# Four selective-scan layers on one core: the side steps of layer 0 in other groups, and one weight set loaded during the first step

## The chip, the core and the metric

The kernel runs on one core of a Trainium2 chip. A core has a matrix engine (PE, with its weight loads shown as PEld), a vector engine (DVE), a scalar engine (ACT), a general engine (POOL) and a queue that issues transfers (SP); each works through its own list of instructions in the order of the program, and they wait for one another through semaphores. The metric is the device time of one execution in microseconds (us), the median of several runs.

## The reference, cut to what matters

Four layers follow one another on images of 192 channels and 48 by 48 pixels, four images, all in 32-bit floats. The change is in layer 0. For each image it runs two pairs of Mamba passes; in a pair one pass reads the 2304 pixels forward, the other backward, and their results are added:

```
xz = u @ inW.T;  xh, z = split(xz);  xc = silu(causal_conv(xh, 3 taps))
xdbl = xc @ xpW.T          # dt (12), B (16), C (16)
delta = softplus(dt @ dtW.T + dtB);  A = -exp(A_log)
h_t = exp(delta_t*A) * h_(t-1) + (delta_t*u_t) * B_t      # 16 states x 384 channels
y_t = sum_n h_t*C_t + xc*D;  out = (y * silu(z)) @ outW.T
layer 0:  m = pair_0(x with rows and columns swapped)
          out = pair_2(layernorm(m swapped back)*w + b + x)
```

Between the two pairs each pixel is normalised over its 192 channels and the input is added. This "mixing" is what the text calls the side steps. Layers 1 to 3 (a convolution block with a four-direction scan, another four-direction scan, a row-wise and column-wise Mamba with an MLP) are not touched by the change.

## The kernel before, in words

**Jobs, steps and groups.** A pass of layer 0 over one image is cut into 6 jobs of 384 pixels (`MambaJob`, `mamba_pass`). Layer 0 has 2 pairs x 4 images x 2 directions x 6 = 96 jobs, and `run_jobs` takes them one after another in one long pipeline. The 384 channels are 3 blocks of 128, the 16 states are 4 groups of 4, so a job has 12 groups; "step n" is the stretch in which the groups of job n are scanned, and "group 0" to "group 11" is the place in it (the variable `at`). One group on DVE is a multiplication `inputs<-du,bcb` and the scan `h<-a,inputs`.

**Who feeds the scan.** ACT makes the decays `a` two groups ahead, into three buffers that rotate, so its four exponentials of group t start when the scan of group t-1 has ended. In groups 3, 7 and 11 it also copies the next channel block's `du` into PSUM, after three of the four exponentials; the next `inputs` on DVE reads that copy. POOL multiplies the scanned `h` by C (`h<-h,bcb`). PE then adds it up in PSUM (`y<-h,ident`, `reduce`), one group later. `h` has three buffers: the scan of group t+3 writes over that of group t.

**Work for the neighbours.** Beside these, a step projects the next job (`units` of `MambaJob`: `inner` and `conv` in groups 0 to 3, B and C in group 5, `delta` in group 7, `z` in groups 9 and 10), and closes the previous one: its output projection in groups 4 and 6, and for a backward job the sum with the forward pass's result (`o<-o,prior`, on POOL, group 8). Each such unit is a PE part and an ACT part with a PSUM buffer of two (`ps`) between them. The functions silu and softplus are in other ACT tables than exp, so these units are framed by table loads.

**Side steps.** `mix` makes, for each backward job of the first pair, a list of steps from `Normed.norm`: two centerings (`ps<-o,center` on PE, then on ACT a copy `nx<-ps` and a square `nsq<-ps`), the variance (`ps<-nsq,mean` on PE, then Ln and Exp on ACT), a scaling on POOL, a load of the input, an affine pair on ACT, and an addition into the turned image on POOL. `Side.slot` starts at most one of them per group, when the group is in the list for its kind; `run_jobs` offers a job's list in group `offered` of the step after the next job's start, and calls `Side.slot` after the units and ahead of `reduce`. So the places of the side steps in each engine's list follow from `offered` and `slots`. There are 24 such jobs, one per backward chunk and image, and their side steps lie in the first half of layer 0.

**Weights.** `PairWeights` holds one direction's weights. `load` issues 7 transfers on SP; `derive` makes `A` and 12 diagonal matrices of 128x128. With `late` false these are DVE instructions; with `late` true they are ACT instructions, handed to a job as `extras` (`load` in group 0, `A` and four matrices in group 8, four in group 9, four in group 11). Before the change both sets of the first pair are loaded and derived ahead of everything, and the second pair's two sets are extras of later jobs.

Of the kernel before, what the change touches and what calls it, by code (L numbers as in the profile page):

```python
# [33 lines left out]
def halves(d):  # L34

    return d.rearrange("(k p) l -> p k l", p=Q)
# [251 lines left out]
class ScanJob:  # L288
# [8 lines left out]
    steps, offered = None, 3  # L297
# [200 lines left out]
class MambaJob(ScanJob):  # L498
# [2 lines left out]

    skips, offered = True, 9

    def __init__(
        self, k, pools, w, c0, rev, prev, src, dst, mirror=False, twin=None, prior=None
# [404 lines left out]
def mamba_pass(k, pools, w, rev, src, dst, mirror=False, prior=None):  # L912
    jobs = []
    for n in range(NCH):
        c0 = (NCH - 1 - n if rev else n) * CH
        prev = jobs[-1] if jobs else None
        jobs.append(MambaJob(k, pools, w, c0, rev, prev, src, dst, mirror, prior=prior))
    return jobs
# [12 lines left out]
def layer0(k, pairs, wh, norm, outs):  # L931

    with ExitStack() as ctx:
        nc = k.nc
        pool = ctx.enter_context(k.tc.tile_pool(name="w", bufs=1))
        one = ctx.enter_context(k.tc.tile_pool(name="s1", bufs=1))
        ws = [[PairWeights(k, pool, p, n, m == 1) for n, p in enumerate(pair)] for m, pair in
              enumerate(pairs)]  # L940
        for w in ws[0]:
            w.load()
            w.derive()
        nw = k.tile(one, [Q, 2, 2], "nw")
        nc.sync.dma_start(nw, norm.rearrange("(k p) v -> p k v", p=Q))
        normed = Normed(k, one, one)
        pools = ScanPools(k, ctx, 1, False)
        slots = {"pe": (1, 9, 11), "pool": (3, 7), "act": (5,), "dma": (0, 4, 8)}
        side = Side(k, pools.ps, slots)
        mixed = [k.dram([C, L], "mixed") for _ in range(B)]  # L950

        def mix(b, job):

            at = L - CH - job.c0
            c = at // CH
            st = {}

            def affine(x, of):
                st["x"] = x
                for m in range(2):  # L960
                    of(x[:, m, :], m)

            def load(sq):
                st["res"] = sq
                nc.sync.dma_start(sq, halves(wh[b])[:, :, at : at + CH])

            def add():
                for m in range(2):
                    k.g.tensor_tensor(
                        rows_of(normed.turned[:, m, :], c),  # L970
                        *(square_rows(st[v][:, m, :]) for v in ("x", "res")),
                        ALU.add,
                    )

            steps = normed.norm(
                lambda: [job.o], 0, nw[:, :, 0], nw[:, :, 1], affine, spare=load
            )
            steps.append(("pool", add))
            return [steps, *(normed.parts(halves(mixed[b]), normed.turned) if c == NCH - 1 else [])]

        jobs = []
        for m, (there, back) in enumerate(ws):
            for b in range(B):
                src = (wh, mixed)[m][b]
                first, out = k.dram([C, L], "first"), outs[b] if m else k.dram([C, L], "sum")
                some = mamba_pass(k, pools, there, False, src, first)
                some += mamba_pass(k, pools, back, True, src, out, True, first)
                if m == 0:
                    for job in some[NCH:]:
                        job.steps = lambda b=b, job=job: mix(b, job)  # L990
                jobs += some

        n = len(jobs) // 2
        for i in range(2):
            jobs[n + i * NCH - NCH + 1].extras = ws[1][i].extras()
        run_jobs(jobs, side)
# [297 lines left out]
def square_rows(ap):  # L1294

    return ap.rearrange("p (r l) -> p r l", l=S)


def rows_of(img, c):

    return img.rearrange("p (w h) -> p h w", h=S)[:, c * RC : (c + 1) * RC, :]
# [338 lines left out]
def network(tc, d, out):  # L1640
    with ExitStack() as ctx:
# [13 lines left out]

        x1 = images("x1")
        layer0(k, [pair(0), pair(2)], [d["x_wh"][b] for b in range(B)], d["L0_norm"], x1)


# [173 lines left out]
```

## Time and profile before

| what | us |
|---|---|
| median of 3 runs (19716.89 to 19721.89) | 19721.09 |
| the profiled execution's own time | 19716.54 |
| its span, from the first instruction to the last | 19714.8 |
| DVE busy | 18084.7 |
| PE busy | 17500.7 |
| POOL busy | 14746.4 |
| ACT busy | 12837.2 |
| first scan of layer 0 starts at | 42.72 |

The profile is of one execution. A busy share is an average over stages with different limits, so the text goes by single groups: the trace's answers give for an instruction its start, its length and, in brackets, the idle time of its engine just before it and what ended that idle time. "DVE inputs <- ACT du" means that `inputs` on DVE waited for the copy of `du` on ACT. Several instructions that follow one another on an engine are shown as one line with a count.

### The profile page before, as it was taken

How to read it: one execution, taken by the hardware profiler on the slowest of the kernel's cores; microseconds unless marked ns; L12 is line 12 of the kernel's file. 1: busy time of each engine (PE TensorE's matmuls, PEld its weight loads, DVE VectorE, ACT ScalarE, POOL GpSimd, SP SyncE). 2: the span in 40 equal slices, each digit the busy share in tenths (PEclk: the TensorE clock that was granted, in tenths of full speed). 3: DMA queues.
4: the chain of work that ended last, by engine and by line, in shares of the span. 5: the costliest groups of instructions: out<-in, count | busy, mean ns of one | idle time of the engine just before them, and what ended most of it. 6: DMA issues, size and time to landing. Idle time of an engine off the chain costs nothing.

```text
span 19714.8 us, 159611 instructions
## 1 busy us (share of the span) xinstructions
PE 17500.7 (89%) x48240; PEld 8295.6 (42%) x48240; DVE 18084.7 (92%) x7310; ACT 12837.2 (65%) x22569; POOL 14746.4 (75%) x10860
## 2 busy tenths in 40 slices
PE   8999999999998878888888888889999999999989
PEld 4444444444444322232233333334444444444444
DVE  8999999999998699999999999969999999999993
ACT  6666667666665466666666766766666666666663
POOL 7888878878776278888888888857777777777770
PEclk9999999999999989999999999999999999999999
DMA  3333333333332366666666666642222322333221
GB/s 113 115 108 116 110 117 117 110 114 106 112 115 88 97 134 138 149 144 148 146 143 145 140 144 144 139 115 105 105 102 105 108 105 104 111 107 106 105 106 46
DMA packets 500475, 2306.35 MB, mean 117 GB/s; under 512 B 76664, under 2 KB 334304, under 8 KB 347168
## 3 DMA queue, kind: packets, MB, share of 16 engines
q1 hardware_dynamic: 499616, 2296.14, 41.2%
q8 instruction: 387, 6.34, 0.1%
q14 instruction: 472, 3.87, 0.1%
HBM read 2103.60 MB, written 192.32 MB: 116 GB/s over the span
## 4 chain that ended last, share of the span: by engine, by line
DVE 39%; POOL 33%; PE 13%; issue 10%; ACT 3%; DMA 2%; DVEq 0%; SPq 0%; POOLq 0%; ACTq 0%
POOL h L56 25%; DVE h L56 25%; DVE inputs L56 13%; PE y L56 5%; PE ps L56 4%; POOL dus L56 3%; PE vps L114 2%; POOL state L56 1%; ACT a L93 1%; DMA bcb<-bc 1%; POOL yt L56 1%; POOL bcb L56 1%; PE mop L114 1%; PE mps L114 1%; ACT L93 1%
## 5 line engine op out<-in xcount | busy, mean ns | idle before, releaser
L56 POOL TENSOR_TENSOR h<-h,bcb 128x1536 f32<-128x1536 f32 x3456 | 11907.7, 3446 | 1704.9 <-DVE h L56 1429.9
L56 DVE TENSOR_TENSOR_SCAN h<-a,inputs 128x1540 f32<-128x1540 f32 (+1 forms) x3456 | 11606.6, 3358 | 440.6 <-ACT a L93 4.1
L93 ACT ACTIVATE a<-delta,A 128x384 f32<-128x384 f32 (+1 forms) x13824 | 7432.2, 602 | 3160.3 <-DVE h L56 3148.7
L56 PE MATMUL y<-h,ident 128*128 128x384 f32 x18432 | 6789.3, 516 | 513.5 <-POOL h L56 510.5
L56 DVE TENSOR_TENSOR inputs<-du,bcb 128x1540 f32<-128x1540 f32 (+1 forms) x3456 | 6114.4, 1769 | 503.7 <-ACT du L93 96.4
L56 PEld LDWEIGHTS y<-h,ident 128*128 128x128 f32 x18432 | 3633.6, 201 | 3517.3 <-POOL h L56 951.9
L56 PE MATMUL y<-h,sum 128*64 128x384 f32 x9216 | 3667.1, 547 | 581.4 <-POOL h L56 461.3
L56 PEld LDWEIGHTS y<-h,sum 128*64 128x64 f32 x9216 | 1292.4, 150 | 2909.0 <-issue 1738.0
L56 POOL COPY state<-h 128x4 f32<-128x4 f32 x2304 | 431.4, 187 | 2228.2 <-DVE h L56 2199.7
L56 PE MATMUL ps<-xh,diag 128*128 128x384 f32 x4032 | 1418.7, 491 | 177.9 <-ACT xc L93 177.9
L56 PE MATMUL ps<-u,inT 96*128 96x384 f32 x3456 | 1249.1, 492 | 155.1 <-ACT z L93 105.9
L56 PE MATMUL ps<-bcd,dtT 12*128 12x384 f32 (+1 forms) x2304 | 1023.8, 552 | 397.4 <-ACT delta L93 394.8
L56 PEld LDWEIGHTS ps<-xh,diag 128*128 128x128 f32 x4032 | 750.4, 189 | 772.7 <-ACT xc L93 266.0
L93 ACT ACT_TABLE_LOAD x794 | 1018.7, 1283 | 14.0
L90 ACT ACT_TABLE_LOAD x789 | 1012.3, 1283 | 14.3 <-PEq L1823 0.7
L56 PEld LDWEIGHTS ps<-u,inT 96*128 96x128 f32 x3456 | 649.4, 191 | 661.6 <-ACT z L93 177.6
L93 ACT ACTIVATE delta<-ps,vec 128x384 f32<-128x384 f32 x1152 | 630.3, 578 | 303.4 <-PE ps L56 296.9
L56 PEld LDWEIGHTS ps<-bcd,dtT 12*128 12x128 f32 (+1 forms) x2304 | 383.7, 192 | 965.8 <-ACT delta L93 631.8
L56 PE MATMUL ps<-yt,outT 128*96 128x384 f32 x2304 | 789.7, 486 | 0.4 <-POOL yt L56 0.4
L93 ACT ACTIVATE du<-dus 128x384 f32<-128x384 f32 x1152 | 558.8, 485 | 164.2 <-DVE inputs L56 158.8
L56 POOL TENSOR_TENSOR dus<-delta,xc 128x384 f32<-128x384 f32 x576 | 574.7, 998 | 51.8 <-ACT delta L93 51.8
L93 ACT ACTIVATE o<-ps 96x384 f32<-96x384 f32 x288 | 140.0, 486 | 684.4 <-PE ps L56 684.4
(131 smaller groups left out, 9702.8 us busy)
## 6 DMA issues: line engine op xcount, KB each, us to landing
bcb<-bc SPq DMA_DIRECT2D x384, 1540.0 KB
bcb<-bc SPq DMA_DIRECT2D x768, 770.0 KB
bcb<-bc SPq DMA_DIRECT2D x384, 1536.0 KB
y<-o SPq DMA_DIRECT2D x192, 288.0 KB
xs<-xi_wh SPq DMA_DIRECT2D x96, 288.0 KB
xs<-xi_hw SPq DMA_DIRECT2D x96, 288.0 KB
added<-y SPq DMA_DIRECT2D x96, 288.0 KB
xs<-x_wh SPq DMA_DIRECT2D x96, 288.0 KB
```

The lines of the kernel that those rows point to most:

```text
L56: return lambda *a, **kw: self.tc.keep_in_program_order(op(*a, **kw))
L90: self.in_order(self.nc.scalar.preload_act_table_set(LOG_EXP))
L93: return self.in_order(self.nc.scalar.activation(out, in_, func, **kw))
L114: (engine or self.nc.tensor).matmul(out, lhsT, rhs, start=start and i == 0, stop=stop and i == n - 1)
```

## The change

Two edits, both in layer 0.

The side steps move: a job's list is offered in group 11 of the step and not in group 9, and steps that begin on PE may start in groups 1, 2 and 11 and not in 1, 9 and 11. The first centering goes from group 9 to group 11, the second from group 11 to group 1 of the next step, the variance from group 1 to group 2. The scaling (group 3), the load (4), the affine pair (5) and the addition (7) stay.

The weights move: of the first pair, only the forward direction's set is loaded and derived ahead of the first job. The backward direction's set becomes `late`, and its `load` and `derive` are extras of the very first job.

```diff
-    skips, offered = True, 9
+    skips, offered = True, 11
...
-        ws = [[PairWeights(k, pool, p, n, m == 1) for n, p in enumerate(pair)] for m, pair in
-              enumerate(pairs)]
-        for w in ws[0]:
-            w.load()
-            w.derive()
+        ws = [
+            [PairWeights(k, pool, p, n, m + n > 0) for n, p in enumerate(pair)]
+            for m, pair in enumerate(pairs)
+        ]
+        ws[0][0].load()
+        ws[0][0].derive()
...
-        slots = {"pe": (1, 9, 11), "pool": (3, 7), "act": (5,), "dma": (0, 4, 8)}
+        slots = {"pe": (1, 2, 11), "pool": (3, 7), "act": (5,), "dma": (0, 4, 8)}
...
         n = len(jobs) // 2
+        jobs[0].extras = ws[0][1].extras()
         for i in range(2):
             jobs[n + i * NCH - NCH + 1].extras = ws[1][i].extras()
```

In the built program the 7 transfers of the second set stand on SP behind the first two loads of `u` and ahead of `bc<-bcd`; DVE has 13 instructions fewer at the start; on ACT the one Exp of the start goes to the first step, and 13 come to it there.

## The prediction

> **What bounds the kernel.** I read the page first: DVE is busy 92% of the span and carries most of the chain that ended last, through `h` and `inputs`.
>
> ```profile
> span 19714.8 us, 159611 instructions
> DVE 39%; POOL 33%; PE 13%; issue 10%; ACT 3%; DMA 2%; DVEq 0%; SPq 0%; POOLq 0%; ACTq 0%
> ```
>
> In layer 0 DVE sets the pace: a group takes 5.35 us, 1.77 of `inputs` and 3.36 of scan. A gain can only come from DVE's idle time, so next I asked for the waits of DVE in the first half of layer 0, 38 to 3263 us, where the side steps lie.
>
> ```profile
> DVE inputs L56 <- ACT du L93: 78.3, 25, 26.0
> DVE inputs L56 <- POOL bcb L56: 21.8, 58, 0.5
> DVE h L56 <- PE y L56: 1.8, 4, 0.5
> ```
>
> One of the 25 waits for `du` is the kernel's start (25.95 us); the other 24 hold 52.3 us, and there are 24 jobs with side steps. In the second half of layer 0, without side steps, the same view lists no wait for `du`. What makes `du` late is in the timeline of one such step (POOL, PE, ACT, DVE, by start):
>
> ```profile
> 677.52 1.80 POOL L56 TENSOR_TENSOR o<-o,prior 96x768 f32<-96x768 f32 x1
> 679.37 1.53 PE L56 MATMUL ps<-o,center 96*96 96x384 f32 x4 [3.30 <-POOL o L56]
> 681.78 4.05 PE L56 MATMUL y<-h,ident 128*128 128x384 f32 x8
> 681.00 0.49 ACT L93 ACTIVATE nx<-ps 96x384 f32<-96x384 f32 x1 [4.96 <-PE ps L56]
> 691.78 0.47 ACT L93 ACTIVATE du<-dus 128x384 f32<-128x384 f32 x1
> 692.34 1.77 DVE L56 TENSOR_TENSOR inputs<-du,bcb 128x1540 f32<-128x1540 f32 x1 [2.23 <-ACT du L93]
> ```
>
> The first centering stands in group 9, but POOL adds up the `o` that it reads behind the `h` of group 8, until 679.32. PE waits 3.30 us, ACT behind it 4.96 us, with the decays and the `z` of group 10 queued behind `nx`. ACT never recovers by group 11, and `du` is 2.23 us late for DVE.
>
> The measure of a step without side steps is one of the second half, around its groups 11 to 3:
>
> ```profile
> 6031.48 2.85 PE L56 MATMUL y<-h,ident 128*128 128x384 f32 x8 [1.21 <-POOL h L56]
> 6047.64 2.85 PE L56 MATMUL y<-h,ident 128*128 128x384 f32 x8 [0.56 <-POOL h L56]
> 6031.06 0.47 ACT L93 ACTIVATE du<-dus 128x384 f32<-128x384 f32 x1
> 6033.06 2.14 ACT L93 ACTIVATE a<-delta,A 128x384 f32<-128x384 f32 x4 [0.99 <-DVE h L56]
> 6043.85 2.13 ACT L93 ACTIVATE a<-delta,A 128x384 f32<-128x384 f32 x4 [2.32 <-DVE h L56]
> 6049.20 1.63 ACT L93 ACTIVATE a<-delta,A 128x384 f32<-128x384 f32 x3 [3.22 <-DVE h L56]
> 6033.23 1.77 DVE L56 TENSOR_TENSOR inputs<-du,bcb 128x1540 f32<-128x1540 f32 x1 [0.20 <-DVE h L56]
> ```
>
> Here `du` ends 1.5 us before the previous scan does, and both PE and ACT have idle time in front of groups 0 to 3. Last, the start: two weight sets on SP ahead of `u`, and PE's first matmul waiting for `u`.
>
> ```profile
> 4.31 0.49 SPq L824 DMA_DIRECT2D xpT<-in_L_xpT  x1
> 9.48 0.82 SPq L523 DMA_DIRECT2D u<-in_x_wh  x2
> 15.02 1.62 PE L56 MATMUL ps<-u,inT 96*128 96x384 f32 x2 [15.02 <-DMA u<-in_x_wh]
> ```
>
> **What the Trainium skill says.** "PSUM — Partial Sum Buffer", section "Engine vs sequencer instructions": the queues of ScalarE, VectorE and GpSimdE are strict FIFO and matmuls start in program order. The trace agrees: decays whose buffer was free at 679.2 start at 681.76, behind `nx`. "TensorE: Matmul & The Clock Gate", section "What's actually happening": an idle window of about 3.4 us halves the array's clock. After the 3.30 us of idle the same eight matmuls took 4.05 us, against 2.75 elsewhere, so the wait costs PE more than itself. "ScalarE: Activation LUTs", section "Table sets": one set holds both ln and exp. In this trace the Ln and Exp of the variance have no table load around them, so moving them adds none.
>
> **The change part by part.**
>
> *The centering leaves group 9.* PE's wait (3.30) and ACT's (4.96) go. ACT then starts group 10's decays at 679.25 and not at 681.76, a gain of 2.5 us; `nx` and `nsq` leave group 9 as well (0.9), and `z` finds its two PSUM buffers unshared. In the measure step `du` is in time with 1.5 us to spare. DVE's next release is then the end of its own scan, with the 0.20 us gap of that step: each of the 24 waits of 52.3/24 = 2.18 shrinks to 0.20, 24 x 1.98 = 47.5 us. In four of these steps the scan of group 10 is also held, by POOL's `state` and PE's late `y` (5.80, 5.78, 5.78 and 5.65 us for the group, not 5.37): 1.5 us more. Sum 49.
>
> *Centering in group 11.* PE: 1.45 us, in the measure step's 1.21 us of idle ahead of `reduce`. ACT: `nx` 0.48 and `nsq` 0.48, in the 0.99 us of idle. The second centering stood there before with the same size. Cost nothing; without the cover, 0.3 us on PE, which has a slack of some 3 us before an `h` buffer is needed.
>
> *Second centering in group 1, variance in group 2.* Group 1 exchanges four matmuls for four (1.45 each) and Ln/Exp (0.58+0.52) for `nx`/`nsq` (0.96). New is group 2: PE 1.45, ACT 1.10. By the measure step: the centering pushes group 1's `reduce` by about 0.5 us (0.37 of idle absorbs the rest), the variance ends near 6048.8, group 2's `reduce` is 1.0 late after its 0.56 of idle, Ln and Exp run 6048.9 to 6050.0. The queue behind them on ACT is group 3's decays, due at 6049.20: 0.8 late. `du` of group 3 then ends near 6052.0, and the scan that it must beat ends at 6054.52: 2.5 us to spare. After the table load the first `xc` is 0.5 late, and PE's third conv with it; `reduce` of group 2 then ends near 6059.3, and the scan that needs its `h` buffer starts at 6061.90. In the built program the second conv waits for the Ln that empties its PSUM buffer, which is already done, so it doesn't queue behind `xc`. Cost nothing; if that cover is used up, each us beyond 2.5 costs 24.
>
> *Queues passed.* POOL's scaling in group 3 now has one group, not two, after Exp; it stands behind the `h` of group 3, which ends near 6058.3, 8 us after Exp. On SP no transfer moves. POOL's own overload in groups 3 and 7 (the 21.8 us) stays.
>
> *The start.* SP drops seven issues ahead of `u`: 4.57 us (from 4.31 to the next transfer at 8.88). What must land ahead of `u` falls by one set, 981 KB or 1.0 MB; from 5 to 15 us the DMA moved some 240 GB/s, so 4.2 us. Bounds: 3.4 us at the 297 GB/s of its best slice, 4.6 by the issues; I take 4.2, as all of the chain to the first scan at 42.72 hangs on the first matmul. The set's transfers then run beside the first projections; SP has nothing to issue from 10.3 to 29.47.
>
> *The late set.* ACT gets 0.23+0.24+12 matrices, 4.6 us, in groups 8, 9 and 11 of the first step. The second pair's set does the same at 3307.58 to 3324.92 in the trace: `du` ended at 3323.21, `inputs` came at 3324.72 with a 0.20 gap. Cost 0. DVE's 13 instructions were off the path: 0.
>
> **Sum.** 47.5 + 1.5 + 4.2 = 53 us. The span goes from 19714.8 to 19661.6, the profiled execution from 19716.54 to 19663. That execution is 4.6 below the median of the runs; 19721 - 53 = **19668**. Of the kernel, 0.27%. About 0.2%, 39 us, is what a measurement of this kernel can tell from no change.
>
> **Rivals.**
>
> *The wait moves to group 3.* In a step with side steps PE is nearly gapless (65.6 of 71.3 us), fuller than the measure step. If PE stays as far behind as before, the variance ends 16.9 us after group 0's `inputs` began, Exp at 18.1, `du` at 20.4, against a scan end at 21.4. One us of slack then; two us more of lag would cost 24 and give 19692. For it: the full PE. Against: the lag came from the idle and the slow clock that go.
>
> *The late `du` is the table loads' doing.* Group 10's `z` with two loads of 1.28 us stands before `du` in every step; then only the start counts: 19717. Against: the measure step has the same loads and is in time.
>
> *Slower.* Ln and Exp hold group 3's decays so long that `du` stalls DVE by more than the change saves: from 53/24 = 2.2 us per step it is no gain, and from 3.8 us it is slower by 39 us, 19760. Exp would have to end 3.8+1.0 to 3.8+2.5 us later than worked. Nothing in the trace is that late there.
>
> **Chances.** The forecast 0.76 (its own range 19656 to 19679), the wait that moves 0.14 (19680 to 19712), table loads 0.06, slower 0.04. Faster by over 0.2% takes the forecast and a little of the second: 0.79; within 0.2%: 0.17; slower 0.04. The range reaches into the second case, to 19692; below, to the start's and the noise's end, 19655.
>
> **What would show it.** In the changed profile: no `nx` wait of 5 us on ACT, no PE wait for POOL `o`, DVE's waits for `du` down to the start's one of about 21.7 us, group 11 at 5.44 us, first scan near 38.5. Waits of DVE for `du` at group 3 or for PE `y` at group 5 would prove me wrong.

## The result

The changed kernel takes **19681.04 us** (median of 17 runs, 19673.69 to 19687.33) against 19720.92 for the kernel before beside it (17 runs, 19714.20 to 19727.93). The ratio is 0.998, 95% interval 0.9973 to 0.9986: 39.9 us faster, with an interval of some 28 to 53 us. The forecast was 53 us faster.

The page of the changed kernel, its span and the chain that ended last by engine:

```profile
span 19683.5 us, 159587 instructions
DVE 43%; POOL 26%; PE 15%; issue 8%; ACT 5%; DMA 1%; DVEq 1%; POOLq 0%; SPq 0%; ACTq 0%
```

The chain still runs through DVE, with a larger share than the 39% of before. Next the same view as in the prediction, the waits of DVE from 38 to 3263 us (total, times, longest, in us):

```profile
DVE inputs L56 <- POOL bcb L56: 22.5, 59, 0.5
DVE inputs L56 <- DVE h L56: 7.7, 37, 0.4
DVE inputs L56 <- POOL state L56: 2.6, 6, 0.5
DVE h L56 <- ACT a L93: 2.4, 3, 1.7
...
DVE h L56 <- PE y L56: 0.4, 1, 0.4
```

No wait for `du` is left in this window, where there were 24 with 52.3 us; POOL's `bcb` is as before (21.8 us, 58 times). The waits of `inputs` for DVE's own scan, most of them the 0.20 us gap that the prediction named, are 37 and not 21 (4.2 us before). The timeline of the same step, groups 9 to 11, shows why:

```profile
670.79 1.83 POOL L56 TENSOR_TENSOR o<-o,prior 96x768 f32<-96x768 f32 x1
672.58 2.13 ACT L93 ACTIVATE a<-delta,A 128x384 f32<-128x384 f32 x4 [1.30 <-DVE h L56]
676.03 1.06 ACT L93 ACTIVATE z<-ps 128x384 f32<-128x384 f32 x2
677.96 2.75 PE L56 MATMUL y<-h,ident 128*128 128x384 f32 x8
678.15 1.77 DVE L56 TENSOR_TENSOR inputs<-du,bcb 128x1540 f32<-128x1540 f32 x1
678.67 1.28 ACT L90 ACT_TABLE_LOAD   x1
680.55 1.45 PE L56 MATMUL ps<-o,center 96*96 96x384 f32 x4
681.50 0.47 ACT L93 ACTIVATE du<-dus 128x384 f32<-128x384 f32 x1
682.42 0.47 ACT L93 ACTIVATE nx<-ps 96x384 f32<-96x384 f32 x1
683.45 2.13 ACT L93 ACTIVATE a<-delta,A 128x384 f32<-128x384 f32 x4 [0.19 <-DVE h L56]
683.62 1.77 DVE L56 TENSOR_TENSOR inputs<-du,bcb 128x1540 f32<-128x1540 f32 x1 [0.20 <-DVE h L56]
```

POOL's `o` is complete at 672.62; the centering that reads it now starts at 680.55, without a wait. ACT's decays of group 10 begin as soon as DVE has released their buffer. `du` ends at 681.97, and DVE's `inputs` follows its own scan with a gap of 0.20 us, where it had waited 2.23.

Then the groups that took in the moved work, 1 to 3 of the following step:

```profile
693.12 0.48 ACT L93 ACTIVATE nsq<-ps 96x384 f32<-96x384 f32 x1
697.69 1.46 PE L56 MATMUL ps<-nsq,mean 96*96 96x384 f32 x4
699.25 0.58 ACT L93 ACTIVATE nsq<-ps,eps 96x384 f32<-96x384 f32 x1 [2.86 <-PE ps L56]
699.86 0.53 ACT L93 ACTIVATE nsq<-nsq 96x384 f32<-96x384 f32 x1
700.28 1.61 ACT L93 ACTIVATE a<-delta,A 128x384 f32<-128x384 f32 x3
701.56 3.36 DVE L56 TENSOR_TENSOR_SCAN h<-a,inputs 128x1540 f32<-128x1540 f32 x1
701.80 0.47 ACT L93 ACTIVATE du<-dus 128x384 f32<-128x384 f32 x1
705.06 1.77 DVE L56 TENSOR_TENSOR inputs<-du,bcb 128x1540 f32<-128x1540 f32 x1
```

Exp (the second `nsq` on ACT after 699) ends at 700.39, and `du` at 702.27, 2.65 us ahead of the end of the scan at 704.92. `inputs` at 705.06 waits for nothing.

Last the start:

```profile
4.83 0.94 SPq L523 DMA_DIRECT2D u<-in_x_wh  x2
5.82 0.45 SPq L824 DMA_DIRECT2D xpT<-in_L_xpT  x1
11.08 6.67 PE L56 MATMUL ps<-u,inT 96*128 96x384 f32 x12 [11.08 <-DMA u<-in_x_wh]
39.47 3.36 DVE L56 TENSOR_TENSOR_SCAN h<-a,inputs 128x1540 f32<-128x1540 f32 x1 [1.73 <-ACT a L93]
```

`u` is issued at 4.83 and not at 9.48, ahead of the second set (`xpT` at 5.82), and the first matmul comes 3.94 us earlier.

That is what was meant, and yet the whole is 13 us short of the forecast. To find where, I cut each span at the first and last scan of layer 0, of layers 1 and 2, and of layer 3. The cuts are the starts of these scans. There are two traces of each kernel; the second is among the experiments below:

| part, us | before | after | mean difference |
|---|---|---|---|
| to the first scan | 42.7, 43.1 | 39.5, 38.8 | -3.8 |
| layer 0, first to last scan | 6247.7, 6243.0 | 6201.6, 6201.0 | -44.1 |
| to the first scan of layer 1 | 476.8, 478.4 | 476.7, 477.3 | -0.6 |
| layers 1 and 2 | 6219.3, 6215.7 | 6225.7, 6227.6 | +9.2 |
| to the first scan of layer 3 | 164.3, 168.2 | 168.6, 167.1 | +1.6 |
| layer 3 | 6102.4, 6103.6 | 6111.6, 6111.0 | +8.3 |
| after the last scan | 461.6, 460.9 | 459.9, 460.7 | -1.0 |

Layer 0 and the start give nearly what was worked out. Some 17 us are lost in layers 1 to 3, whose code is the same in both kernels. In layer 3 the waits of DVE say where. This view of the kernel before, from just after layer 3's first scan to its last:

```profile
DVE h L56 <- ACT a L93: 0.5, 1, 0.5
```

and of the changed kernel, in the same stretch:

```profile
DVE h L56 <- ACT a L93: 3.9, 8, 0.5
DVE h L56 <- DVE inputs L56: 2.9, 6, 0.5
DVE inputs L56 <- DVE h L56: 2.3, 5, 0.5
DVE h L56 <- PE ps L56: 1.0, 2, 0.5
DVE h L56 <- PE y L56: 0.5, 1, 0.5
```

One stop became 22, each of 0.44 to 0.50 us. They are put down to ACT, to PE and to DVE itself, so no single one of these can be behind them; the releaser named is whatever ended last before. One of them in the timeline of DVE in the changed kernel:

```profile
13205.50 1.77 DVE L56 TENSOR_TENSOR inputs<-du,bcb 128x1536 f32<-128x1536 f32 x1
13207.40 3.35 DVE L56 TENSOR_TENSOR_SCAN h<-a,inputs 128x1536 f32<-128x1536 f32 x1
13210.79 1.77 DVE L56 TENSOR_TENSOR inputs<-du,bcb 128x1536 f32<-128x1536 f32 x1
13213.04 3.35 DVE L56 TENSOR_TENSOR_SCAN h<-a,inputs 128x1536 f32<-128x1536 f32 x1 [0.48 <-PE ps L56]
```

From the end of the second `inputs` to its scan are 0.48 us, where the first pair has 0.13; the stop costs the difference, 0.35. I compared these places with DVE's list of instructions in the built program, semaphore instructions included. All 22 stand at an index that leaves 64 when divided by 128, and so does the single stop of before. Both kernels pass such an index every 128 instructions, 37 times in layer 3; what differs is what stands there:

| layer 3, at such an index | before | after |
|---|---|---|
| scans, with a stop | 1 of 1 | 17 of 17 |
| multiplications, with a stop | 0 of 11 | 5 of 7 |
| semaphore instructions | 25 | 13 |

At a semaphore instruction no idle time of DVE shows, and at a multiplication it may or may not; a scan always shows it, in layers 0 to 2 too. The change takes 13 instructions from DVE's start (14988 become 14975), so every later instruction has another index.

### The profile page after: what moved, and what is told of

It reads as the page before. It is cut to its first block, busy times and chain, and to the rows that moved or that the text cites. A ratio compares the mean times of both kernels' runs of the same rounds, so it can differ in the third digit from the quotient of the medians.

```text
span 19683.5 us, 159587 instructions
## 1 busy us (share of the span) xinstructions
PE 17478.0 (89%) x48240; PEld 8281.7 (42%) x48240; DVE 18085.6 (92%) x7297; ACT 12836.3 (65%) x22582; POOL 14746.8 (75%) x10860
## 4 chain that ended last, share of the span: by engine, by line
DVE 43%; POOL 26%; PE 15%; issue 8%; ACT 5%; DMA 1%; DVEq 1%; POOLq 0%; SPq 0%; ACTq 0%
DVE h L56 28%; POOL h L56 20%; DVE inputs L56 15%; PE y L56 7%; PE ps L56 5%; POOL dus L56 2%; ACT a L93 2%; PE vps L114 2%; POOL state L56 1%; ACT L93 1%; PE mop L114 1%; DMA bcb<-bc 1%; POOL yt L56 1%; PE mps L114 1%; POOL bcb L56 1%
## 5 line engine op out<-in xcount | busy, mean ns | idle before, releaser
L90 ACT ACT_TABLE_LOAD x789 | 1012.3, 1283 | 14.7 <-PEq L1825 0.7
```

The source lines that it names most:

```text
L90: self.in_order(self.nc.scalar.preload_act_table_set(LOG_EXP))
```

## The experiments

**Theory A**: layer 0 and the start gain what was worked out, and the loss in layer 3 goes by the index of DVE's instructions. **Theory B**: the loss comes from elsewhere, such as the changed start or the changed timing of layer 0. Beside the first four runs the kernel before took 19720.59 us (38 runs); beside the next four 19718.13 (44 runs).

### The side steps alone

```diff
-    skips, offered = True, 9
+    skips, offered = True, 11
-        slots = {"pe": (1, 9, 11), "pool": (3, 7), "act": (5,), "dma": (0, 4, 8)}
+        slots = {"pe": (1, 2, 11), "pool": (3, 7), "act": (5,), "dma": (0, 4, 8)}
```

> The kernel before with the side steps moved alone (offered in group 11, PE groups 1, 2 and 11); the weights as before. Theory A (the gain of layer 0 is the waits for du, and the change gave some 9 us of it back in later layers because DVE has 13 instructions fewer: at every 128th instruction of its list DVE loses 0.35 us, seen only where it is a multiplication or a scan and not an event wait; 35 such places before, 60 after): this kernel has DVE's count of before, so the whole 46 to 48 us of the side steps show, 19674, and layer 3 is as long as before. Theory B (the later layers' 9 us are scatter, or a consequence of the side steps): 19684. Theory C (the table loads make du late): 19721.

Measured: 19681.25 us (15 runs, 19672.76 to 19687.37), ratio 0.9979 (0.9971 to 0.9986). Layer 0's scans take 6201.6 us and layer 3's 6104.8 with one stop, as A says. The total doesn't speak for A: it is 7 us above A's figure and 3 below B's. In this trace the first scan starts at 46.3 and layers 1 and 2 take 6228.2, which was neither edited nor expected. The second trace below takes this up. The count of places was also off: in layers 0 to 3 the kernel before has 43 multiplications and scans at such an index, not 35, and 32 of them show a stop.

### The weights alone

```diff
-        for w in ws[0]:
-            w.load()
-            w.derive()
+        ws[0][0].load()
+        ws[0][0].derive()
...
+        jobs[0].extras = ws[0][1].extras()
```

(with the second set of the first pair `late`, as in the change)

> The kernel before with the weight set alone made late; the side steps as before. First scan 3.2 us earlier under every theory. Theory A: 13 DVE instructions fewer cost 25 x 0.35 = 8.8 us in all layers together, so it is slower, 19726. Theory B: 3.2 us faster, 19718. Forecast of the prediction: 4.2 faster, 19717.

Measured: 19725.27 us (13 runs), ratio 1.0003 (0.9995 to 1.0012). The first scan starts at 38.2, 4.5 us earlier than before, and the run isn't faster. Layer 3 takes 6112.2 us and its waits are those of the changed kernel, line for line, with 22 stops. So it is this edit that brings them, and they spend its gain.

### One and two memsets more

```diff
+        spare = k.tile(one, [Q, 1], "spare")
+        for i in range(1):
+            nc.vector.memset(spare[:, i : i + 1], 0.0)
```

This adds to the changed kernel one DVE instruction at the start, or two (`[Q, 2]`, `range(2)`), which nothing reads.

> The changed kernel with one more DVE instruction at the start, a memset of a column nobody reads, while DVE waits anyway. Theory A: of the places at every 128th instruction 41 fall on a multiplication or a scan and not 60, so 19 x 0.35 = 6.7 us faster than the changed kernel, 19674; layer 3 has some 11 of the stops and not 22. Theory B: the same as the changed kernel, 19681.

> The changed kernel with two more DVE instructions at the start. Theory A: 65 places on a multiplication or scan, not 60, so 1.7 us slower than the changed kernel, 19683, and some 8 us slower than with one instruction. Theory B: the same as with one, 19681.

Measured: one memset more gives 19670.57 us (8 runs), ratio 0.9974 (0.9964 to 0.9984), and two give 19679.31 (13 runs), 0.9979 (0.9971 to 0.9987). With one instruction added the kernel is 10 us faster, though medians with such intervals do not prove it. The traces settle where it comes from: with one memset layer 3 takes 6104.8 us with one stop, with two 6110.9 with 18, each at an index of the same remainder. The stops follow the index, not the work.

That two are some 8 us slower than one came true (8.7), but A's other sizes missed: one memset came out 3 us below the 19674 and left one stop in layer 3, not some 11; two came out 4 us below the 19683. The forecasts had counted every multiplication and scan at such an index, and not every multiplication stops. The stops that show in layers 0 to 3, counted afterwards, are 58 in the changed kernel, 29 with one memset and 54 with two. At 0.35 us each that is 10.2 and 1.4 us less than the changed kernel; the medians are 10.5 and 1.7 less.

### The weights alone, with the count of before

```diff
+        spare = k.tile(one, [Q, 13], "spare")
+        for i in range(13):
+            nc.vector.memset(spare[:, i : i + 1], 0.0)
```

on top of the weights' edit.

> The weights' edit alone, with 13 memsets of one column put on DVE at the start in place of the 13 instructions that the edit takes from it, so that every later instruction of DVE has the index it has in the kernel before. Theory A (the time of layers 1 to 3 goes by the index of DVE's instructions): layer 3's scans take 6102 to 6105 us as in the kernel before, with 1 visible stop and not 22, and the start's 4 us are no longer given back: 19717, that is 8 less than the weights' edit alone at 19725.3. Theory B (the loss of layers 1 to 3 comes from elsewhere, the start's other order of transfers for one): layer 3's scans stay at 6112 us and the time at 19725.

Measured: 19714.78 us (13 runs), ratio 0.9998 (0.999 to 1.0006). Again the times alone can't tell it from no change. The trace can: the first scan stays early, at 38.0, layer 3 takes 6103.6 us and not 6112.2, and its waits are one line, that of the kernel before:

```profile
DVE h L56 <- ACT a L93: 0.5, 1, 0.5
```

The order of transfers and the late set are those of the weights' edit; only the count is that of before. Theory B falls for layer 3.

### The centering in group 10

```diff
-    skips, offered = True, 9
+    skips, offered = True, 10
-        slots = {"pe": (1, 9, 11), "pool": (3, 7), "act": (5,), "dma": (0, 4, 8)}
+        slots = {"pe": (1, 10, 11), "pool": (3, 7), "act": (5,), "dma": (0, 4, 8)}
```

> The kernel before with the first centering one group later, in group 10, by which POOL has long added up the o that it reads; the second centering stays in group 11, the variance in group 1. Theory A (the stall is PE's wait for POOL's o): the waits of DVE for du in layer 0 go from 52 us to below 10, and the time to 19680, give or take 5. Rival (the table loads around z, or the side steps' own work of 1.45 us on PE and 0.96 on ACT ahead of du, make du late): the centering still stands ahead of du with all of its work, so the waits stay at some 50 us and the time at 19720.

Measured: 19689.13 us (21 runs), ratio 0.9985 (0.9979 to 0.9992); layer 0 takes 6217.4 us. Neither side has it. The waits for `du` beyond the start's 26.1 are 19.9 us: 21 of some 0.95 us, not below 10 and not 50.

```profile
DVE inputs L56 <- ACT du L93: 46.0, 22, 26.1
```

The step's timeline, groups 10 and 11:

```profile
681.25 1.77 DVE L56 TENSOR_TENSOR inputs<-du,bcb 128x1540 f32<-128x1540 f32 x1
682.62 0.49 ACT L93 ACTIVATE nx<-ps 96x384 f32<-96x384 f32 x1 [0.86 <-PE ps L56]
683.00 0.48 ACT L93 ACTIVATE nsq<-ps 96x384 f32<-96x384 f32 x1
683.50 1.28 ACT L90 ACT_TABLE_LOAD   x1
684.79 1.63 ACT L93 ACTIVATE a<-delta,A 128x384 f32<-128x384 f32 x3
686.33 0.47 ACT L93 ACTIVATE du<-dus 128x384 f32<-128x384 f32 x1
686.88 1.77 DVE L56 TENSOR_TENSOR inputs<-du,bcb 128x1540 f32<-128x1540 f32 x1 [0.38 <-ACT du L93]
```

`nx` waits 0.86 us for PE, and with `nsq` holds the table load until 683.50, 2.25 us after the group's `inputs` at 681.25. In the changed kernel nothing stands between `z` and the load, which came 0.52 after `inputs` (678.15 and 678.67). These 1.73 us make `du` late again. So one group later wins 28 of layer 0's 44 us; the other 16 are what the place between `z` and the load costs in group 10.

### The centering in its old place, but not reading `o`

```diff
+        nc.gpsimd.memset(normed.turned, 1.0)
...
-                lambda: [job.o], 0, nw[:, :, 0], nw[:, :, 1], affine, spare=load
+                lambda: [normed.turned[:, :, :CH]], 0, nw[:, :, 0], nw[:, :, 1], affine, spare=load
```

> The kernel before with every step in its old group, but the centering reads a tile that was filled once at the start and not the job's o; so the normalisation of layer 0 isn't that of o: the dependence on POOL is left out, all of the work stays. Theory A (the wait for POOL's o is the cause): PE no longer waits in group 9, the waits of DVE for du go from 52 us to below 10, time 19678 give or take 5. Rival (the work of the centering in group 9 itself is the cause): waits of 50 us, 19720.

Measured: 19678.88 us (11 runs), ratio 0.9979 (0.997 to 0.9988). Layer 0 takes 6201.4 us, and of the waits for `du` beyond the start's 24.0 two are left, with 2.2 us together:

```profile
DVE inputs L56 <- ACT du L93: 26.2, 3, 24.0
```

The 1.45 us of PE and 0.96 us of ACT are still in group 9, with the same table loads after them. POOL's additions write the tile that is read in place of `o`, but PE waits for it nowhere in this half of layer 0. Gone are the dependence on POOL's `o` and the waits of PE that it brought, which the kernel before shows between 38 and 3263 us as

```profile
PE ps L56 <- POOL o L56: 53.2, 24, 3.3
```

and the whole of layer 0's gain is there. The dependence is the cause; in group 9 the work itself has room.

### POOL's scaling in two halves

The changed kernel with one memset more, and:

```diff
-        slots = {"pe": (1, 2, 11), "pool": (3, 7), "act": (5,), "dma": (0, 4, 8)}
+        slots = {"pe": (1, 2, 11), "pool": (3, 4, 7), "act": (6,), "dma": (0, 5, 8)}
...
-                else [("pool", scale_both), ("dma", lambda: spare(st["sq"]))]
+                else [
+                    ("pool", lambda: scale(0)),
+                    ("pool", lambda: scale(1)),
+                    ("dma", lambda: spare(st["sq"])),
+                ]
```

> The changed kernel with one memset more on DVE at the start (19670.6), and in it POOL's scaling of 3.5 us in group 3 cut into its two halves, one in group 3 and one in group 4; the load then starts in group 5 and the affine pair in group 6. Theory: what is left in the mixing steps of layer 0 over 5.35 us a group is POOL's overload behind the scaling (group 4, some 3.5 us over all steps) and the addition (groups 8 and 9, 10 us); halving the scaling takes 3 to 4 us away: 19667. Rival (POOL's backlog is only spread over two groups): 19670.6, within 1.

Measured: 19669.61 us (10 runs), ratio 0.9975 (0.9965 to 0.9984). The times can't tell 19667 from 19670.6: the ten runs lie between 19665.96 and 19678.17. The trace can: layer 0 takes 6200.7 us, against 6200.2 without the split. Nothing is won, as the rival says, with a twist:

```profile
DVE inputs L56 <- POOL bcb L56: 13.9, 34, 0.5
...
DVE h L56 <- PE y L56: 7.3, 8, 2.0
```

The waits for `bcb` fall by 9.0 us from the 22.9 of the kernel without the split, and 7.3 us of waits for PE's `y`, of which that kernel has none here, come up in their place.

### A second trace of four kernels

No edit; the same programs once more, in one execution each.

> The kernel before once more, for a second trace of the same program. If the stops of DVE go by the index of its instructions, layer 3's scans have 1 visible stop and take 6102 to 6105 us again. If the start and the waits for du of layers 1 and 2 (18 us, and 13.9 to 28.2 over ten traces) are scatter of an execution, the first scan (42.7) may differ by a few us and those waits by up to 10, with no change of the code; if they belong to the program, both stay within 1 us.

> The changed kernel once more. By the index of the instructions: layer 3's scans show 22 visible stops again and take 6111 to 6113 us; layer 0's take 6201 to 6202. Waits for du of layers 1 and 2 (27 us before): scatter lets them fall to as little as 14; if they belong to the program they stay within 1 us of 27.

> The side steps' edit alone once more. By the index: layer 3 has 1 visible stop and takes 6102 to 6105 us; layer 0's scans 6201 to 6202. If scatter: the first scan comes nearer to the kernel before's 42.7 than to 46.3, and layers 1 and 2 nearer to 6219 than to 6228; if they belong to this program, 46.3 and 6228 again.

> The changed kernel with one memset more, once more. By the index: layer 3 has 1 visible stop and takes 6103 to 6105 us, layer 0's scans 6200 to 6202. If scatter, the waits for du of layers 1 and 2 (17.6 us) may differ by up to 10; if they belong to the program they stay.

Layer 3 repeats with its stops: 6103.6 us with one (before), 6111.0 with 22, at the same 22 instructions (changed), 6104.8 with one (side steps alone), 6104.9 with one (one memset more). Layer 0 repeats where the side steps moved: 6201.0, 6201.1 and 6200.1. In the kernel before it takes 6243.0, not 6247.7, with 47.3 us of waits for `du` and not 52.3.

What does not repeat is the surplus of the side steps' edit. Its first scan starts at 42.8 (46.3 in the first trace), and its layers 1 and 2 take 6216.2 us (6228.2), with 9.7 us of waits for `du` there (24.9). In its first trace PE's first twelve matmuls took 8.02 us, in the second 6.09. So the surplus comes and goes between executions of one program. The two took 19682.92 and 19675.53 us, and the median of its runs, 19681.25, lies nearer the first; why more of them lie there is not shown. In the other kernels too these waits moved: 18.1 and 10.2 us before, 27.5 and 25.0 changed, 17.6 and 14.7 with one memset. For the changed kernel layers 1 and 2 are 6225.7 and 6227.6, for the kernel before 6219.3 and 6215.7. All three traces of the weights' edit without a memset lie between 6225.7 and 6228.7, but two of the eleven others do as well (6228.2 for the side steps alone, 6228.0 for the run that doesn't read `o`). Both kernels have 17 visible stops in these layers. Both traced executions of the changed kernel took 19685.3 us, 4.3 above its median, those of the kernel before 19716.54 and 19714.60, 4.4 and 6.3 below its own; on average that is 9.6 us between them, about the surplus. This speaks for scatter. Whether some of the +9 us belongs to the change is open.

## Why the prediction was right, and where it was not

**Right in sign, in the whole range and in most of the mechanism; 53 us forecast, 39.9 measured.** The time lies 2 us outside the range that the forecast gave itself (19656 to 19679), in that of the rival with the wait in group 3 (19680 to 19712), and that wait did not come. So it was in part luck that the whole range, to 19692, held it: a loss nobody had thought of took the room left for another. Layer 0's gain of 44.1, the start's 3.8 and layer 3's loss of 8.3 add up to 39.6. The two pairs of traces also hold 9.2 us of loss in layers 1 and 2, so that their spans differ by 30.2 us. The median doesn't need these 9; at its interval it can't exclude them.

**The step that failed: "DVE's 13 instructions were off the path: 0".** They were off the path, and their removal still cost 8.3 us in layer 3; 21 stops more at 0.35 us each make 7.4 of them. In layer 0 19 stops show and not 14, 1.8 us at 0.35 each. Group by group the changed kernel and the side steps alone do differ there by 0.34 to 0.37 us at 31 of the 33 places where only one of them stops, but in the sum other differences hide it: 6201.6 and 6201.0 us with 19 stops, 6201.6 and 6201.1 with 14. I had asked what waits for these instructions and not what their absence does to all that follow. This is the largest miss.

**The waits for `du`: 47.5, mis-sized.** The mechanism is shown: the waits went, and they went as well with the dependence on `o` alone. But 52.3 us was one execution. The other three traced executions with layer 0's side steps in their old places and reading `o` have 47.3 (the kernel before again), 48.1 and 44.8 (the weights' edit with and without memsets). At their mean of 48.1 with the first the same sum gives 24 x (2.01 - 0.20) = 43.3, and with 1.5 for group 10 44.8 (43.0 if the five stops are taken off), against 44.1 measured.

**The slow clock.** The prediction had the slow clock go with the wait. It is tied to it in part. In the trace of before, each of the 17 waits of PE for `o` of 1.94 us and more has a stretch of 3.4 or 6.8 us at a granted clock of 0.5 that begins within 1.7 us of the wait's end (681.0 to 684.4 in the step shown); none of the seven of up to 1.0 us has one. But between 38 and 3263 us the half clock falls only from 273 us to 218, so most of it has other grounds, and DVE's waits for `du` went all the same.

**The start: 4.2.** The first matmul came 3.9 us earlier in the first pair of traces and 3.8 in the second; the first scan 3.8 on average. The sign I named for it was wrong, though: DVE's first wait for `du` was to fall from 25.95 to about 21.7, and it grew to 28.3. DVE reaches `inputs` earlier because its 12 matrices and one `A` are gone, so the length of the wait does not tell when the scan starts.

**The other costs put at nothing.** They held. From group 0's `inputs` to the end of Exp I had worked out 16.8 us, and the trace has 16.77 (683.62 to 700.39); the slack of `du` in group 3 was to be 2.5 and is 2.65. The late set in the first step costs DVE nothing: that step takes 63.88 us, as the unburdened job 6 does.

**The rivals.** The wait that moves to group 3 needed an Exp 18.1 us after `inputs` for its lag, and is out by the 16.77. The table loads alone are out by the run in which the loads and all the work stay and the waits go. They are not without part: with the centering in group 10, what stands ahead of the load makes `du` late by 0.95 us in 21 steps, which my forecast for that run missed. The slower case is out: group 11 takes the 5.44 us that was named, and no `du` is late in group 3.

**Order and place in a list.** The strict order within an engine (the Trainium skill, "PSUM — Partial Sum Buffer", section "Engine vs sequencer instructions") carried the explanation, and the changed trace agrees: with no `nx` ahead of them, group 10's decays start at 672.58, as soon as their buffer is free, where they had stood behind `nx` until 681.76. On the stops, the Trainium skill, "Runtime: NRT & Kernel Launch", section "Instruction fetch mechanics", says that instructions are fetched ahead in blocks of 256 and that the cost of crossing from one block to the next is mostly hidden. The trace shows a stop of 0.35 us at a period of 128 instructions, so something tied to the place in the list is not hidden here. That it is the fetch is an inference from the period; no run shows it.

## What to carry to other kernels

When work waits in an engine's list for a late partner, count all that is queued behind it: the 3.3 us of PE and 5 us of ACT cost DVE 2 us a step only by delaying a copy two groups on, and moving the reader by one group gave two thirds, by two groups all. When an edit changes the number of instructions on the engine that sets the pace, compare the untouched parts of the two traces as well; a loss scattered over code that didn't change, in equal small stops with ever other releasers, may go by the place in the list, and one idle instruction more can win it back (19670.57 us here, the changed kernel being at 19681.04). Size a stall from more than one execution where it is to be known to a tenth.

## What was not expected of the hardware

DVE lost about 0.35 us at places of its own list whose index leaves 64 when divided by 128: at every scan there, with a gap of 0.48 us ahead of it in place of 0.13, at some multiplications (5 of 7, or 0 of 11, in layer 3), and visibly at no semaphore instruction. In layer 3 such places fall mostly on scans or hardly ever, by how many instructions stand ahead: 22 stops in the changed kernel, 1 with one memset more, 18 with two, 1 in the kernel before. The same stops came back at the same instructions in a second execution.

Between two executions of one program the first scan moved by up to 3.5 us (46.3 and 42.8), and the waits for `du` in layers 1 and 2 by 15 (24.9 and 9.7), with 12 us between the lengths of these layers. A single trace of this kernel can't settle a difference below some 12 us in those parts.
